# Four attention layers on one NeuronCore: the output projections and last stores of layers 2 and 3 moved into the branches, and eight additions of layer 1 handed to GpSimd

## The chip, the cores and the metric

The kernel runs on one core of a Trainium2 chip, in one launch. The metric is the device time in microseconds (us). Of the kernel before there are three runs: 3575.72, 3578.60 and 3578.97 us, median 3578.6. The profiled execution took 3578.05 us, and its profile spans 3576.3 us. All times below that are written as a position, such as 3514.46, are microseconds from the start of that span.

## The reference

An image x of shape (2, 512, 32, 32) goes through four layers. All data is float32. Only the ends of layers 1, 2 and 3 matter here:

```python
# layer 1: linear attention, residual
matrix_sum = v_sum[:, :, None] + jnp.einsum('bnm,bmc->bcn', Qt, matrix)
x = x + gamma[0] * (matrix_sum * tailor[:, None, :]).reshape(b, c, h, w)

# layers 2 and 3: group norm, q/k/v, attention of 8 heads of 64, projection, residual
xn = group_norm(x)                       # 8 groups in layer 2, 32 in layer 3
qkv = einsum('oc,bcn->bon', qkv_w, xn) + qkv_b
attn = softmax(q^T k * scale)            # per head, 1024 x 1024
out = einsum('bhnm,bhcm->bhcn', attn, v)
x = x + einsum('oc,bcn->bon', proj_w, out) + proj_b
```

## The kernel before

x stays on chip for the whole kernel: eight tiles `xs[b][t]` of 128 channels by 1024 positions, for two batches b and four channel blocks t. A "half" h below is 512 of the 1024 positions.

**Layer 0** (up to about 2107 us) is a deformable attention with a small network evaluated for each pair of positions, and then a two-matrix MLP (up to 2547 us). The change touches it only in names. One function of it, `share`, matters for the reading of the profile: it accumulates in one PSUM tile `acc` of 128 x 2 x 512 float32, writes half 0 with TensorE, has VectorE add it to x (line 202), and writes half 1.

**Layer 1** ends with 16 products, one for each batch, half and channel block (line 774), each 128 x 512 in PSUM. VectorE adds each to x (line 778). VectorE also takes the statistics for layer 2's group norm, two `bn_stats` for each tile of x (line 906) and one aggregation (907), for both batches, before layer 2's first product of q and k (848) can start.

**Layers 2 and 3** run through `attention`. `queries_keys_values` computes the group norm, q, k and v, and a flag that says whether the logits are small. Then the program branches at run time: `heads_bounded` does the softmax without a maximum, `heads_general` is the fallback. The data here take the bounded branch. In it, TensorE's order is written out by hand: 16 units (batch, pair of heads, half) of eight steps. In each step TensorE makes scores `s` (956), ScalarE takes the exponential (960), TensorE multiplies by v into `o` (985). VectorE and GpSimd add the exponentials up (965 to 974). At the end of a unit `divide` multiplies the sums by a matrix of ones into `d` (1002). ScalarE copies one half of `d` (1006), VectorE adds the other (1007), takes the reciprocal (1008) and scales the result q (1010). `divide` for a unit is called four steps into the next unit; for the last unit it is called after the last product by v, with nothing behind it in the branch.

After the branch, in code that both branches share, `project` runs 16 projections (batch, output block o, half): four matmuls of 128x128 by 128x512 into a one-bank PSUM tile `pb` (line 585; four such tiles rotate), and one VectorE instruction that adds bias and x (589). Each float32 matmul shows as two records in the profile. In layer 2 the statistics of layer 3's group norm (906, 907) stand in the same stretch of code, so they are placed between those additions. In layer 3, `epilogue` stores each tile of x once both halves are done (line 87, eight stores of 512 KB).

Outside the hand-written stretches a scheduler places instructions in each engine's queue, within one block of straight code; it does not move them across a branch. Waits between engines are semaphores. The program tracks a tile as a whole when it decides what has to wait for what.

Of the kernel before, what the change touches and what calls it, by code (L numbers as in the profile page):

```python
# [11 lines left out]
F32 = mybir.dt.float32  # L12
AF = mybir.ActivationFunctionType
ALU = mybir.AluOpType
# [4 lines left out]
P = 128  # L19
B, C, H, W = 2, 512, 32, 32  # L20
N = H * W
CT = C // P
# [25 lines left out]
class Net:  # L48
# [16 lines left out]
    def prologue(self, ctx: ExitStack):  # L65
# [13 lines left out]
                self.xs[b].append(xt)  # L79
        self.ident = const.tile([P, P], F32, tag="ident", name="ident")  # L80
        make_identity(nc, self.ident)

    def epilogue(self, out: bass.AP):
        y = out.rearrange("b (t p) h w -> b t p (h w)", p=P)
        for b in range(B):
            for t in range(CT):
                self.nc.sync.dma_start(y[b, t], self.xs[b][t])

# [7 lines left out]
    def layer0(self):  # L98
# [3 lines left out]
        with ExitStack() as ctx:  # L102
# [27 lines left out]
            with self.tc.manual_schedule(engines=engines):  # L130
                pairs = [{} for _ in range(BP)]
                for n, _ in enumerate(self.offsets(pairs[0], 0, ps)):
                    if n == 4:
                        self.fold_weights()
                front = [self.sampled(pairs[0], 0, ps)]
                after, sims, att = [], {}, None
                tables = {}
                quads = [(u, o, jj) for u in range(2 * BP) for o in range(8) for jj in range(2)]
                ready = self.first_hidden(*quads[0], pairs, tables)
                held, self.join = [], None  # L140
                for i, (u, o, jj) in enumerate(quads):
                    if o == 1 and jj == 1 and u % 2 == 0 and u // 2 + 1 < BP:
                        nxt = pairs[u // 2 + 1]
                        front += [self.offsets(nxt, u // 2 + 1, ps), self.sampled(nxt, u // 2 + 1, ps)]
                    h1 = ready
                    if i + 1 < len(quads):
                        if quads[i + 1][1:] == (7, 0) and u + 1 < 2 * BP:
                            self.advance(front, lambda: "logs" in pairs[(u + 1) // 2])
                        ready = self.first_hidden(*quads[i + 1], pairs, tables)
                    z = self.second_hidden(u, o, jj, h1, i + 1 == len(quads))  # L150
                    if jj == 1:
                        held.append((u, o, (first, z)))
                    else:
                        first = z
                        if len(held) == 2:
                            v, last, zs = held.pop(0)
                            self.last_product(v, last, zs, sims, ps_s)
                            if last == 7:
                                if v % 8 == 0:
                                    self.advance(after, lambda: False)  # L160
                                    att = [
                                        apool.tile([P, N], F32, tag=f"att{t}", name=f"att{v}_{t}") for t in range(CT)
                                    ]
                                self.advance(front, lambda: "v" in pairs[v // 2])
                                after.append(self.attend(v, pairs[v // 2], sims.pop(v), att, ps))
                                if v % 8 == 7:
                                    after.append(self.projection(ps, att, ow, v // 8))
                    self.step(after)
                    self.step(front)

                self.join(True)
                self.advance(after, lambda: False)
                self.last_product(*held[0], sims, ps_s)
                accs = [ps.tile([P, 2, HF], F32, tag="ps", name=f"ob{o}") for o in range(CT - 1)]
                share = self.share(accs, att, ow)
                next(share)
                self.last_product(*held[1], sims, ps_s)
                for n, _ in enumerate(self.attend(u, pairs[u // 2], sims.pop(u), att, None)):
                    if n in (0, 1):
                        next(share)  # L180
                for _ in share:
                    pass
                for h in range(2):
                    self.project_one(ps, att, ow, "out_b", B - 1, CT - 1, h)

    def share(self, accs, att, w):

# [63 lines left out]
    def projection(self, ps, att, ow, b):  # L251
        for o in range(CT):
            for h in range(2):
                self.project_one(ps, att, ow, "out_b", b, o, h)
                yield

    def offsets(self, m, bt, ps):
# [312 lines left out]
            nc.vector.tensor_copy(to[rows, HF:N], sim[rows, :])  # L570
        yield

    def project(self, ps, att, w, bias: str, b: int):

        for o in range(CT):
            for h in range(2):
                self.project_one(ps, att, w, bias, b, o, h)

    def project_one(self, ps, att, w, bias: str, b: int, o: int, h: int):
        nc = self.nc  # L580
        cut = slice(h * HF, (h + 1) * HF)
        acc = ps.tile([P, HF], F32, tag="ps", name=f"{bias}_{b}{o}{h}")
        for t in range(CT):
            wt = w[t] if isinstance(w, list) else w[:, t, :]
            nc.tensor.matmul(  # L585
                acc, lhsT=wt[:, o * P : (o + 1) * P], rhs=att[t][:, cut], start=(t == 0), stop=(t == CT - 1)
            )
        xt = self.xs[b][o][:, cut]
        nc.vector.scalar_tensor_tensor(xt, acc, self.col(bias, o), xt, ALU.add, ALU.add)
# [58 lines left out]
    def layer1(self, w, bias):  # L648
# [3 lines left out]
        with ExitStack() as ctx:  # L652
            pool = self.pool(ctx, "l1")
            small = self.pool(ctx, "l1s", 3)
            ps_t = self.pool(ctx, "l1_ps_t", 3, psum=True)
            ps_m = self.pool(ctx, "l1_ps_m", 1, psum=True)
            ps = self.pool(ctx, "l1_ps", 3, psum=True)
# [111 lines left out]
            for b in range(B):  # L769
                for h in range(2):  # L770
                    cut = slice(h * HF, (h + 1) * HF)
                    for t in range(CT):
                        w_ps = ps.tile([P, HF], F32, tag="ps", name=f"w{b}{h}{t}")
                        nc.tensor.matmul(
                            w_ps, lhsT=mats[b][:, t * P : (t + 1) * P], rhs=q_at[2 * b + h], start=True, stop=True
                        )
                        xt = self.xs[b][t][:, cut]
                        nc.vector.tensor_tensor(xt, w_ps, xt, ALU.add)

# [11 lines left out]
            proj.append(wt)  # L793
        return qkv, proj

    def attention(self, k: int, qkv, proj):
        nc = self.nc
        with ExitStack() as ctx:
            one = self.pool(ctx, f"a{k}")
            vb = one.tile([P, C], F32, tag="vb", name=f"vb{k}")  # L800
            nc.sync.dma_start(vb, self.io[f"l{k}_vb"].partition_broadcast(P))
            ones = one.tile([P, DH], F32, tag="ones", name=f"ones{k}")
            nc.vector.memset(ones, 1.0)
            data = []
            for b in range(B):
                qs = [one.tile([P, N], F32, tag=f"q{b}{t}", name=f"q{k}{b}{t}") for t in range(CT)]
                ks = [one.tile([P, N], F32, tag=f"k{b}{t}", name=f"k{k}{b}{t}") for t in range(CT)]
                v = one.tile([P, NB, C], F32, tag=f"v{b}", name=f"v{k}{b}")
                data.append((qs, ks, v))
            small_logits = self.queries_keys_values(k, qkv, vb, ones, data)  # L810

            with self.tc.If(small_logits > 0) as cmp:
                self.heads_bounded(k, ones, data)
            with cmp.Else():
                self.heads_general(k, data)
            with ExitStack() as ctx2:
                ps = self.pool(ctx2, f"a{k}_ps_p", 4, psum=True)
                for b in range(B):
                    self.project(ps, data[b][0], proj, f"pb{k}", b)

    def queries_keys_values(self, k, qkv, vb, ones, data):

# [107 lines left out]
            xn.append(xt)  # L930
        return xn

    def heads_bounded(self, k, ones, data):

# [4 lines left out]
        with ExitStack() as ctx:  # L941
# [72 lines left out]
            with self.tc.manual_schedule(engines={mybir.EngineType.PE}):  # L1014


                for i in range(len(steps) + 5):
                    if i < len(steps):
                        score(*steps[i])
                    for j in ([], [i - 3, i - 2])[i % NB == 3] if i % NB in (2, 3) else [i - 2]:  # L1020
                        if 0 <= j < len(steps):
                            value(*steps[j])
                    if i % NB == 4 and i > NB:
                        divide(steps[i - NB][0])

    def heads_general(self, k, data):
        with ExitStack() as ctx:
# [75 lines left out]
def conv_seq_kernel(ctx: ExitStack, tc: tile.TileContext, io: dict[str, bass.AP], out: bass.AP):  # L1103
# [3 lines left out]
    with tc.tile_pool(name="w_at", bufs=CT) as wpool:  # L1107
# [3 lines left out]
            l2 = net.attention_weights(wpool, 2)  # L1111
            net.layer1(*l1)
        net.attention(2, *l2)
        net.attention(3, *net.attention_weights(wpool, 3))
    net.epilogue(out)

# [107 lines left out]
```

## Time and profile before

| stretch, us | what runs | TensorE busy, us |
|---|---|---|
| 2546 to 2598 | layer 1 up to its last products | 50.6 of 52 |
| 2598 to 2624 | layer 1's additions, layer 2's group norm | 17.2 of 26 |
| 2624 to 2795 | layer 2: q, k, v | 168.9 of 171 |
| 2795 to 3037 | layer 2: heads | 236.1 of 242 |
| 3037 to 3099 | layer 2: projection, layer 3's group norm | 58.0 of 62 |
| 3099 to 3272 | layer 3: q, k, v | 170.5 of 173 |
| 3272 to 3514 | layer 3: heads | 235.4 of 242 |
| 3514 to 3576 | layer 3: projection, last store | 57.1 of 62 |

The table says how much of each stretch TensorE spent on matmuls; what is left over is time in which it waited. TensorE is the engine that is nearly always busy (3497.6 of 3576.3 us), so a change here acts on the time only through what it adds to, or takes from, TensorE's waits at the seams between these stretches, and through what follows the last matmul.

### The profile page before, as it was taken

Reading aid. Unit: us, or ns where it says so; the run is one execution under the profiler, and the core shown is the slowest. Engines: PE = TensorE matmul, PEld = TensorE weight load, DVE = VectorE, ACT = ScalarE, POOL = GpSimd, SP = SyncE. Lnnn points to the kernel's source line nnn. Section 1 sums busy time; section 2 is a strip of 40 time slices with the busy share of each in tenths; the row PEclk is TensorE's granted clock in tenths of the full one; section 3 lists DMA queues with packets and bytes.
Section 4 is the critical chain, followed back from the end, with each engine's and each line's share of the span. In section 5 each row is a group of like instructions: output and inputs, shape, how many; then the busy total and the mean of one; then the engine's idle time right before and its main releaser. Section 6 shows DMA issues by size and latency. Waiting matters only on the chain.

```text
span 3576.3 us, 58840 instructions
## 1 busy us (share of the span) xinstructions
PE 3497.6 (98%) x25184; PEld 1248.3 (35%) x25184; DVE 2023.0 (57%) x2075; ACT 1976.3 (55%) x2003; POOL 1869.8 (52%) x1392
## 2 busy tenths in 40 slices
PE   7999999999999999999999999999999999999998
PEld 2322332332323332332333334444644333443333
DVE  6877777767767668768766620000242467423674
ACT  5877787877776677777777720011010465102661
POOL 4878777787786687887788810000011344012441
PEclk9999999999999999999999999999999999999999
DMA  5777777787786687787888740000000000000001
GB/s 154 152 144 154 153 152 146 151 162 144 153 160 120 125 161 145 151 159 145 167 163 161 146 162 0 0 0 0 1 3 0 36 1 3 15 0 1 1 1 48
DMA packets 101799, 334.70 MB, mean 94 GB/s; under 512 B 12561, under 2 KB 14225, under 8 KB 100241
## 3 DMA queue, kind: packets, MB, share of 16 engines
q0 software_dynamic: 73296, 266.90, 39.4%
q1 hardware_dynamic: 27216, 61.82, 5.6%
q8 instruction: 202, 3.31, 0.4%
q10 hardware_dynamic: 1008, 2.06, 0.2%
q14 instruction: 77, 0.62, 0.1%
HBM read 59.40 MB, written 4.46 MB: 18 GB/s over the span
## 4 chain that ended last, share of the span: by engine, by line
PE 94%; DVE 5%; issue 1%; ACT 0%; POOL 0%; DMA 0%; DVEq 0%; ACTq 0%
PE hp L476 47%; PE m L619 6%; PE m L628 6%; PE s L956 6%; PE o L985 6%; PE qk0p L848 3%; PE pb L585 3%; PE qk1p L848 3%; PE sim L508 3%; PE vp L889 3%; DVE h L445 2%; DVE prod L278 1%; PE out_b L585 1%; PE d L1002 1%; DVE conv L291 1%; PE ob L193 1%
## 5 line engine op out<-in xcount | busy, mean ns | idle before, releaser
L476 PE MATMUL hp<-h,w 128*32 128x512 f32 x16384 | 1825.1, 593 | 7.4 <-DVE h L445 5.9
L445 DVE CUSTOM_DVE_ANT_1 h<-tx,bank 128x1024 f32<-128x1024 f32 x1024 | 1180.9, 1215 | 344.8 <-PE hp L476 321.7
L481 ACT ACTIVATE h<-hp,magb 128x1024 f32<-128x1024 f32 x1024 | 1123.7, 1112 | 437.1 <-PE hp L476 436.1
L476 PEld LDWEIGHTS hp<-h,w 128*32 128x32 f32 x16384 | 529.6, 110 | 1233.2 <-issue 1151.6
L468 POOL DMA_DIRECT2D h<-h x509 | 452.7, 1026 | 406.7 <-ACT h L487 348.5
L494 POOL TENSOR_TENSOR h<-h,h 128x1024 f32<-128x1024 f32 x255 | 614.6, 2410 | 21.3
L492 POOL TENSOR_SCALAR h<-h,flip 128x1024 f32<-128x1024 f32 x256 | 448.9, 1754 | 0.9 <-ACT h L481 0.9
L960 ACT ACTIVATE e<-s 128x1024 f32<-128x1024 f32 x256 | 258.7, 1024 | 152.7 <-PE s L956 152.6
L483 ACT ACTIVATE h<-h,flip 128x1024 f32<-128x1024 f32 x256 | 291.3, 1138 | 0.0
L956 PE MATMUL s<-q,k 64*64 64x512 f32 x2048 | 259.9, 590 | 5.1 <-ACT e L960 3.4
L985 PE MATMUL o<-e,v 64*64 64x512 f32 x2048 | 260.8, 592 | 0.0
L659 POOL MEMSET l1ones<- 128x128 f32 x1 | 0.2, 205 | 476.0 <-PE m L628 476.0
L623 ACT ACTIVATE mh<-m,cols 128x512 f32<-128x512 f32 x64 | 44.0, 687 | 336.5 <-PE m L619 336.5
L619 PE MATMUL m<-mx,w 128*128 128x512 f32 x512 | 220.5, 592 | 0.9 <-issue 0.9
L628 PE MATMUL m<-mh,w 128*128 128x512 f32 x512 | 220.4, 592 | 0.0
L967 POOL TENSOR_TENSOR some<-some,e 128x1024 f32<-128x1024 f32 x64 | 151.3, 2364 | 82.5 <-ACT e L960 80.0
L636 DVE SCALAR_TENSOR_TENSOR x<-m,cols,x 128x512 f32<-128x512 f32 x16 | 12.0, 750 | 318.0 <-PE m L628 318.0
L485 POOL TENSOR_SCALAR h<-h,flip 128x1024 f32<-128x1024 f32 x128 | 154.5, 1207 | 64.0 <-ACT h L481 62.8
L965 POOL TENSOR_TENSOR some<-e,e 128x1024 f32<-128x1024 f32 x32 | 75.9, 2371 | 212.6 <-ACT q L994 139.2
L862 POOL TENSOR_TENSOR sq<-q 128x1024 f32<-128x1024 f32 x16 | 30.3, 1894 | 280.3 <-DVE q L856 280.3
L860 ACT ACTIVATE k<-qk1p,cols 128x512 f32<-128x512 f32 x32 | 22.0, 687 | 245.0 <-PE qk1p L848 245.0
L487 ACT ACTIVATE h<-h,flip 128x1024 f32<-128x1024 f32 x128 | 145.6, 1138 | 0.0
(206 smaller groups left out, 2708.0 us busy)
## 6 DMA issues: line engine op xcount, KB each, us to landing
h<-h POOLq DMA_DIRECT2D x509, 512.0 KB, 6.5
lb<-logs SPq DMA_DIRECT2D x63, 512.0 KB, 5.2
w<-in_mlp_w SPq DMA_DIRECT2D x8, 1024.0 KB, 11.7
qkv<-in_l_qkv SPq DMA_DIRECT2D x8, 768.0 KB, 5.7
x<-in_x SPq DMA_DIRECT2D x8, 512.0 KB, 9.6
out<-x SPq DMA_DIRECT2D x8, 512.0 KB, 2.6
proj<-in_l_proj SPq DMA_DIRECT2D x8, 256.0 KB, 5.9
l1w<-in_l_w SPq DMA_DIRECT2D x1, 1280.0 KB, 8.2
```

The lines of the kernel that those rows point to most:

```text
L445: self.nc.vector._custom_dve(TENSOR_ADD_SAT, out=h[:, k, :, :], in0=x[:, jj, 2 * r + k, :].unsqueeze(1).to_broadcast([P, H, W]), in1=y[:, ...
L468: nc.gpsimd.dma_start(to, what, accum_op=ALU.add)
L476: nc.tensor.matmul(hp[rows, cut], lhsT=self.l0w2[:, 32 * q : 32 * q + 32], rhs=h1[k][:, cut], start=True, stop=True)
L481: nc.scalar.activation(y, hp, AF.Relu, bias=self.magb[:, q : q + 1])
L483: nc.scalar.activation(ys[0], ys[0], AF.Copy, scale=self.flip[:, 0:1])
L492: nc.gpsimd.tensor_scalar(y, y, self.flip[:, 2:3], 1.0, ALU.mult, ALU.mult)
L494: (nc.vector if final else nc.gpsimd).tensor_tensor(y, y, ys[2], ALU.add)
L619: nc.tensor.matmul(acc, lhsT=w1[t][:, o * P : (o + 1) * P], rhs=xn[t], start=(t == 0), stop=(t == CT - 1))
L628: nc.tensor.matmul(acc, lhsT=w2[t // 4][:, t % 4, o * P : (o + 1) * P], rhs=hs[t], start=(t == 0), stop=(t == nh - 1),)
L956: nc.tensor.matmul(s[halves[c], par, :], lhsT=ks[p][rows, at : at + DH], rhs=qs[p][rows, cut], start=True, stop=True)
L960: nc.scalar.activation(e, s, AF.Exp)
L985: nc.tensor.matmul(o[halves[par], r, :], lhsT=v[rows, n, at : at + DH], rhs=e[rows, par, :], start=(n == 0), stop=(n == NB - 1),)
```

## The change

It does four things:

1. Layer 1: for batch 1, ScalarE copies each product out of PSUM into one of four buffers `ws`, and GpSimd adds it to x. Batch 0 stays on VectorE. This relieves VectorE, which both adds and takes statistics there.
2. Layers 2 and 3: the projection moves from behind the branch into both branches, so that it can follow the heads without a jump in between.
3. In the bounded branch the first projection block (batch 0, output block 0, both halves) runs ahead of the last `divide`, whose sums are then given time to become ready; batch 0 does not need that last unit.
4. Each projection block takes one PSUM tile of two halves, from the two buffers that the scores use, instead of two one-bank tiles from a set of four. The last stores are issued half by half (16 of 256 KB) in the branch.

```diff
     def project_one(self, acc, att, w, bias, b, o, h):     # acc is now passed in
-        acc = ps.tile([P, HF], F32, tag="ps", name=f"{bias}_{b}{o}{h}")
...
+    def project_block(self, acc, att, w, bias: str, b: int, o: int, out):
+        for h in range(2):
+            cut = slice(h * HF, (h + 1) * HF)
+            self.project_one(acc[:, h, :], att, w, bias, b, o, h)
+            if out is not None:
+                self.nc.sync.dma_start(out[b, o][:, cut], self.xs[b][o][:, cut])
...
 # layer1
+            last = self.pool(ctx, "l1w", 4)
...
-                        nc.vector.tensor_tensor(xt, w_ps, xt, ALU.add)
+                        if b == 0:
+                            nc.vector.tensor_tensor(xt, w_ps, xt, ALU.add)
+                        else:
+                            ws = last.tile([P, HF], F32, tag="ws", name=f"ws{h}{t}")
+                            nc.scalar.copy(ws, w_ps)
+                            nc.gpsimd.tensor_tensor(xt, xt, ws, ALU.add)
...
 # attention
             with self.tc.If(small_logits > 0) as cmp:
-                self.heads_bounded(k, ones, data)
+                self.heads_bounded(k, ones, data, proj, out)
             with cmp.Else():
                 self.heads_general(k, data)
-            with ExitStack() as ctx2:
-                ps = self.pool(ctx2, f"a{k}_ps_p", 4, psum=True)
-                for b in range(B):
-                    self.project(ps, data[b][0], proj, f"pb{k}", b)
+                with ExitStack() as ctx2:
+                    ps = self.pool(ctx2, f"a{k}_ps_p", 2, psum=True)
+                    for b in range(B):
+                        for o in range(CT):
+                            acc = ps.tile([P, 2, HF], F32, tag="ps", name=f"pbg{k}{b}{o}")
+                            self.project_block(acc, data[b][0], proj, f"pb{k}", b, o, out)
...
 # heads_bounded, behind the loop over steps
-                    if i % NB == 4 and i > NB:
+                    if i % NB == 4 and NB < i < len(steps):
                         divide(steps[i - NB][0])
+                for b in range(B):
+                    for o in range(CT):
+                        acc = ps_s.tile([P, 2, HF], F32, tag="s", name=f"pb{k}{b}{o}")
+                        self.project_block(acc, data[b][0], proj, f"pb{k}", b, o, out)
+                        if b == o == 0:
+                            divide(units[-1])
```

More of the change, by code (lines that the diff above doesn't have):

```diff
@@ L81, in prologue @@
         make_identity(nc, self.ident)
-    def epilogue(self, out: bass.AP):
-        y = out.rearrange("b (t p) h w -> b t p (h w)", p=P)
-        for b in range(B):
-            for t in range(CT):
-                self.nc.sync.dma_start(y[b, t], self.xs[b][t])
     def bn(self, pool, which: str):
@@ L183, in layer0 @@
                 for h in range(2):
-                    self.project_one(ps, att, ow, "out_b", B - 1, CT - 1, h)
+                    acc = ps.tile([P, HF], F32, tag="ps", name=f"out_b_end{h}")
+                    self.project_one(acc, att, ow, "out_b", B - 1, CT - 1, h)
     def share(self, accs, att, w):
@@ L253, in projection @@
             for h in range(2):
-                self.project_one(ps, att, ow, "out_b", b, o, h)
+                acc = ps.tile([P, HF], F32, tag="ps", name=f"out_b{b}{o}{h}")
+                self.project_one(acc, att, ow, "out_b", b, o, h)
                 yield
@@ L571, in attend, with project_one @@
         yield
[L573 to L579, printed above, removed]
+    def project_block(self, acc, att, w, bias: str, b: int, o: int, out):
[4 more added lines that the diff above has]
+                self.nc.sync.dma_start(out[b, o][:, cut], self.xs[b][o][:, cut])
+    def project_one(self, acc, att, w, bias: str, b: int, o: int, h: int):
         nc = self.nc
         cut = slice(h * HF, (h + 1) * HF)
-        acc = ps.tile([P, HF], F32, tag="ps", name=f"{bias}_{b}{o}{h}")
         for t in range(CT):
@@ L794, in attention_weights, with attention @@
         return qkv, proj
-    def attention(self, k: int, qkv, proj):
+    def attention(self, k: int, qkv, proj, out=None):
         nc = self.nc
@@ L812, in attention @@
             with self.tc.If(small_logits > 0) as cmp:
-                self.heads_bounded(k, ones, data)
+                self.heads_bounded(k, ones, data, proj, out)
             with cmp.Else():
                 self.heads_general(k, data)
-            with ExitStack() as ctx2:
-                ps = self.pool(ctx2, f"a{k}_ps_p", 4, psum=True)
-                for b in range(B):
-                    self.project(ps, data[b][0], proj, f"pb{k}", b)
+                with ExitStack() as ctx2:
[4 more added lines that the diff above has]
+                            self.project_block(acc, data[b][0], proj, f"pb{k}", b, o, out)
     def queries_keys_values(self, k, qkv, vb, ones, data):
@@ L931, in group_norm, with heads_bounded @@
         return xn
-    def heads_bounded(self, k, ones, data):
+    def heads_bounded(self, k, ones, data, proj, out):
         nc = self.nc
@@ L1113, in conv_seq_kernel @@
         net.attention(2, *l2)
-        net.attention(3, *net.attention_weights(wpool, 3))
-    net.epilogue(out)
+        net.attention(3, *net.attention_weights(wpool, 3), out.rearrange("b (t p) h w -> b t p (h w)", p=P))
 def _per_partition(v):
```

## The prediction

> **What bounds the kernel now.** I read the chain of waits on the page first, then the timeline at the four seams the edit touches, then the granted clock there. The chain:
>
> ```profile
> PE 94%; DVE 5%; issue 1%; ACT 0%; POOL 0%; DMA 0%; DVEq 0%; ACTq 0%
> ```
>
> TensorE (PE) carries 94% of it, and the number of matmuls does not change. So I price only the time in which TensorE stands still. End of layer 3's heads, by the timeline:
>
> ```profile
> 3505.21 2.75 PE L985 MATMUL o<-e,v 64*64 64x512 f32 x24
> ...
> 3510.44 1.09 PE L1002 MATMUL d<-sum,ones 64*64 64x512 f32 x8 [2.47 <-DVE sum L974]
> 3511.59 0.59 ACT L1006 COPY r<-d 128x512 f32<-128x512 f32 x1 [2.98 <-PE d L1002]
> 3512.21 0.69 DVE L1007 TENSOR_TENSOR r<-d,r 128x512 f32<-128x512 f32 x1 [1.23 <-ACT r L1006]
> 3512.94 3.35 DVE L1008 RECIPROCAL r<-r 128x512 f32<-128x512 f32 x1
> 3514.46 6.05 PE L585 MATMUL pb<-q,proj 128*128 128x512 f32 x9 [2.94 <-issue]
> ```
>
> Two holes: 2.47 us for the last sum, then 2.94 that nothing in the program explains ("issue"), across the jump to the shared code. And nine records take 6.05 us where the steady pace is 0.43 each (one projection, eight records, is 3.43: its additions at L589 come every 3.43). The clock, by stretches (columns: the stretch, its length, busy time and count of TensorE, weight loads, VectorE, ScalarE and GpSimd, then the granted clock, the DMA share and GB/s):
>
> ```profile
> 3514.00:3516.00 2.00, 1.54 (x2) 0.84 (x3) 2.00 (x1) 0.00 (x0) 0.00 (x0) 0.50 0.04 12
> 3516.00:3518.00 2.00, 2.00 (x3) 0.67 (x2) 0.98 (x2) 0.00 (x0) 0.00 (x0) 0.50 0.01 4
> 3518.00:3520.00 2.00, 2.00 (x6) 0.98 (x5) 0.00 (x0) 0.00 (x0) 0.00 (x0) 0.90 0.01 4
> ```
>
> After the holes the clock is 0.50 for some 4 us; 3514.46 to the first addition at 3520.12 is 5.66 us for 3.43 of work. Layer 2's seam shows the same: sum wait 2.47, issue 1.73, slow start.
>
> From layer 2 to layer 3, statistics of x lie between the additions and cost nothing:
>
> ```profile
> 3090.53 0.75 DVE L589 SCALAR_TENSOR_TENSOR x<-pb,cols,x 128x512 f32<-128x512 f32 x1 [1.71 <-PE pb L585]
> 3091.31 0.69 DVE L906 BATCH_NORM_STATS2 stats<-x 128x6 f32<-128x512 f32 x1
> ...
> 3099.41 5.49 PE L848 MATMUL qk0p<-xn,qkv 128*128 128x512 f32 x6 [1.93 <-ACT xn L929]
> ```
>
> The projection's matmuls end at 3093.93, so that seam is 5.5 us. Last, layer 0's `share` accumulates two halves in one tile, as the edit's blocks will:
>
> ```profile
> 2090.68 1.13 PE L193 MATMUL ob<-att,ow 128*128 128x512 f32 x2 [0.66 <-ACT att L569]
> 2091.84 0.75 DVE L202 SCALAR_TENSOR_TENSOR x<-ob,cols,x 128x512 f32<-128x512 f32 x1 [1.06 <-PE ob L193]
> 2092.65 1.98 PE L193 MATMUL ob<-att,ow 128*128 128x512 f32 x4 [0.84 <-DVE x L202]
> ```
>
> TensorE stops 0.84 us before half 1, until VectorE has read half 0, though the halves are different columns.
>
> [...] here 2.36 us (L967) against 1.23 (L974) for 128x1024.
>
> **The change, part by part.** H is the end of the heads' last product (3030.99 in layer 2, 3507.96 in layer 3), P the end of the projection's matmuls.
>
> *Heads to P.* Removed from TensorE's path, layer 3: 2.47 + 2.94 + 2.2 of slow clock (5.66 - 3.43) = 7.6 us. Layer 2: 2.47, a d that takes 1.80 for 1.09 (0.7), 1.73, and 3036.99 to 3043.01 for 3.43 (2.6) = 7.5.
> Added: in the built program's order every half 1 waits on VectorE and, from the third block on, no half 0 does. That is consistent only with half 1 waiting for the addition of half 0 of its own block, as in `share`. Eight blocks at 0.84 = 6.7 us a layer. In the second block it is longer. From H: half 0 to 3.43, stall to 4.27, half 1 to 7.70, d to 8.57, half 0 of block 1 to 12.00. VectorE's queue holds L1007 and L1008 ahead of that block's first addition: 8.57 + 0.6 (ACT) + 0.7 + 3.4 = 13.3, addition to 14.06, half 1 from 14.12. Stall 2.12. So block 1 ends at 17.55, and six blocks of 6.87 + 0.84 bring P to H + 63.8. Before it was 3571.60 - 3507.96 = 63.6 in layer 3 and 62.9 in layer 2. Net **+0.2 and +0.9**: the holes are traded for stalls. The sum, ready 2.43 after H, is hidden by half 0; the last scaling of q (14.8) is first needed in the fifth block, at H + 33. What queues behind half 1's wait on TensorE is the rest of the projection, so each stall goes straight into P. The 16 stores issue from an idle queue beside it.
>
> *Layer 2 to layer 3.* The statistics now lie behind the branch, all after the last addition. VectorE: jump 2.8 to 3.9 us from its last dispatch (ACT took 2.75 from L1006 to its next instruction, TensorE 4.0 from d to pb); I take first statistics at P + 3.3. Eight `bn_stats` and four aggregations: at layer 1's end four and two took 2.51 (2613.05 to 2615.56), so 5.0, to P + 8.3. Then the group norm's chain, by the rows of the seams before: 0.8 over the mean product to its copy (L909, L911), 0.75 for three steps of the variance (2623.74 to 2624.48), 0.6 over the variance product to L919 (2618.62 to 2619.24), 0.9 over the root to the first xn (3096.38 to 3097.30), 2.1 over ScalarE's bias to the product (3097.30 to 3099.41): P + 13.4 against 5.5. TensorE waits through it, where before all but the chain's last part lay beside the projection. And TensorE's order puts one matmul of batch 0 there, then the mean product of batch 1, which needs batch 1's statistics; VectorE does these after four xn (2.98) and seven more `bn_stats` (4.7). That gives P + 19.5 for the second matmul. With 0.4 for the variance product and the clock still at half rate for about three matmuls (1.72 each), the first eight matmuls end near P + 27.6. Before: 3099.41 + 10.09 = P + 15.6, slow clock included. **+12.0.** Bounds: +9 if the jump is hidden[...].
>
> *Layer 1 to layer 2.* VectorE loses 8 additions of about 0.66 (L778). GpSimd's 128x512 addition isn't in the trace. From below, half of 2.36 is 1.18; from above, VectorE's addition is 1.23 for 128x1024 and 0.69 for 128x512, half and 12%, so 1.4. I take 1.2. The first product of batch 1 ends at 2606.2 (2598.43 and nine times 0.86), the copy (0.6, as L994) lies on a ScalarE idle there, the first addition starts near 2607.05, and eight end at 2616.7. What queues behind them is VectorE: the statistics of batch 1 wait for GpSimd, and behind those waits stand the steps of batch 0's norm (mean copy, variance), on which the first q product depends. TensorE's order also puts both variance products ahead of that product now; before, batch 1's lay behind it. From 2616.7: last statistics to 2617.4, variance product and scale of batch 0 to 2619.3, first xn at 2619.6 against 2620.89. **-1.0** with margin rounded off; at 1.4 the additions end 1.6 later, +0.5.
>
> *End.* The last store is half as large. 512 KB land in 2.6 us, so I take 2.3: -0.3. VectorE's jump,[...] ends 2.0 to 3.1 us after the last addition, against that. **0**, bounds -0.3 and +0.6.
>
> Sum: 0.2 + 0.9 + 12.0 - 1.0 + 0 = +12.1: **3590.7 us**, 0.34% slower.
>
> **The rivals.** (a) As intended: no half waits, no exposed statistics: -7.5 - 7.5 - 1.0 = -16, 3562.6. For it: the holes are real. Against: `share` shows the wait, and statistics cannot cross a branch. Chance 5%. (b) Statistics exposed, but no half-tile stall: -1.0 + 12.0 + (0.9 - 6.7 - 1.3) + (0.2 - 6.7 - 1.3) = -3.9, 3574.7, no measurable change. Against it again `share`. 7%. (c) Stalls as priced, but the seam costs half ([...] batch 1's statistics short of blocking): +6, 3584.6. 10%. (d) The same as my forecast, with [...] a cold clock for longer: +17, 3595.6. 8%. My forecast: 70%.
>
> **How the numbers follow.** The forecast's own bounds are 3586 to 3594. Leaving out (a) and (b) leaves 12%; the range is 3582 to 3596 with (c) and (d). The line for "slower" is 3585.8: forecast and (d) are above, (c) mostly within 0.2%. Slower 0.80, same 0.14, faster 0.06.
>
> **What would show it.** Right: L589's line of waits shows pb waiting 0.8 us on VectorE once a block, 2.1 in the second; no "issue" ahead of pb and its clock at 1.0; `bn_stats` of layer 3 in one run behind the last addition, and about 13 us without projections or q products; a second hole of 4 to 5 us after the first q matmul. Wrong: halves of a block back to back, or statistics among the additions.

## The result, and the profile after

The changed kernel takes 3596.95 us (median of 6 runs, 3595.27 to 3598.37); the kernel before, in runs beside it, 3576.85 us. The ratio is 1.0055, with a 95% interval of 1.0042 to 1.0068: half a per cent slower. The two profiles span 3595.5 and 3576.3 us, 19.2 apart. The forecast was 3590.7 us with a range of 3582 to 3596, so the direction was right and the cost was put too low.

The chain of waits of the kernel after says that the bound is the same engine. TensorE's share is a point smaller than before, and "issue" (time in which an engine waits for nothing that the profile shows) has fallen from 1% to 0%:

```profile
PE 93%; DVE 5%; POOL 1%; ACT 0%; issue 0%; DMA 0%; DVEq 0%; ACTq 0%
```

The heads' end in layer 2, TensorE alone, in the timeline of the kernel after (start, duration, engine, line, operation, count, and in brackets the idle time ahead of it with what ended it):

```profile
3027.58 2.75 PE L994 MATMUL o<-e,v 64*64 64x512 f32 x24
3030.27 3.70 PE L583 MATMUL pb<-q,proj 128*128 128x512 f32 x8
3034.81 3.70 PE L583 MATMUL pb<-q,proj 128*128 128x512 f32 x8 [0.85 <-DVE x L587]
3038.44 1.09 PE L1011 MATMUL d<-sum,ones 64*64 64x512 f32 x8
3039.46 3.70 PE L583 MATMUL pb<-q,proj 128*128 128x512 f32 x8
3044.92 7.13 PE L583 MATMUL pb<-q,proj 128*128 128x512 f32 x16 [1.76 <-DVE x L587]
3052.90 7.13 PE L583 MATMUL pb<-q,proj 128*128 128x512 f32 x16 [0.84 <-DVE x L587]
```

The intended gain is there: the projection follows `o` without a hole, the product of ones `d` takes 1.09 us and waits for nothing, and the granted clock is 1.00 from 3028 to 3044. The price stands in the brackets. Eight records, one half of a block, run; TensorE stops until VectorE has read that half; then half 1 of this block and half 0 of the next run as one row of 16. In the second block VectorE is busy with the reciprocal when half 0 is done, so the stop is 1.76 us, as VectorE's timeline of the kernel after shows:

```profile
3040.94 3.35 DVE L1017 RECIPROCAL r<-r 128x512 f32<-128x512 f32 x1
3044.21 0.65 DVE L587 SCALAR_TENSOR_TENSOR x<-pb,cols,x 128x512 f32<-128x512 f32 x1
```

Over the kernel, the list of TensorE's waits puts this line first (us in total, times, longest):

```profile
PE pb L583 <- DVE x L587: 15.3, 16, 1.8
```

Sixteen waits: eight blocks in each of two layers, 14 of 0.84 or 0.85 and two of 1.76.

"Jump" stands below for an engine's passage from the end of the branch to the code that both branches share. At the seam from layer 2 to layer 3 the timeline of the kernel after shows, on VectorE, the jump (2.83 us) and then the statistics in one run,

```profile
3096.53 0.75 DVE L587 SCALAR_TENSOR_TENSOR x<-pb,cols,x 128x512 f32<-128x512 f32 x1 [3.79 <-PE pb L583]
3100.11 1.29 DVE L915 BATCH_NORM_STATS2 stats<-x 128x6 f32<-128x512 f32 x2 [2.83 <-issue]
```

and on TensorE the wait that they cause, and the second one:

```profile
3092.79 3.70 PE L583 MATMUL pb<-q,proj 128*128 128x512 f32 x8 [0.85 <-DVE x L587]
3106.07 0.56 PE L918 MATMUL gm<-mv,avg 128*128 128x4 f32 x2 [9.58 <-DVE mv L916]
3107.47 0.59 PE L926 MATMUL gv<-dv,avg 128*128 128x4 f32 x2 [0.85 <-DVE dv L924]
3111.12 2.08 PE L857 MATMUL qk0p<-xn,qkv 128*128 128x512 f32 x2 [3.06 <-ACT xn L938]
3117.11 0.59 PE L918 MATMUL gm<-mv,avg 128*128 128x4 f32 x2 [3.91 <-DVE mv L916]
3119.69 6.60 PE L857 MATMUL qk0p<-xn,qkv 128*128 128x512 f32 x12
```

TensorE waits 9.58 us for the first mean product `gm`, whose input is the end of the statistics, and 3.91 us for that of batch 1. In the kernel before, the same stretch on TensorE was

```profile
3028.24 2.75 PE L985 MATMUL o<-e,v 64*64 64x512 f32 x24
3036.99 56.93 PE L585 MATMUL pb<-q,proj 128*128 128x512 f32 x128 [1.73 <-issue]
3099.41 10.09 PE L848 MATMUL qk0p<-xn,qkv 128*128 128x512 f32 x16 [1.93 <-ACT xn L929]
```

So the 19.2 us divide as follows. H is the end of the heads' last product and P the end of the projection, as in the prediction; "q" is the end of the first eight calls (matmuls of the program, two records each) of layer 3's q product, where the next row begins: 3109.33 before, 3126.12 after.

| stretch | before, us | after, us | difference | predicted |
|---|---|---|---|---|
| start of the span to H of layer 2 | 3030.99 | 3030.33 | -0.7 | -1.0 |
| H to P, layer 2 | 62.94 | 66.16 | +3.2 | +0.9 |
| P to q | 15.40 | 29.63 | +14.2 | +12.0 |
| q to H of layer 3 | 398.63 | 398.63 | 0.0 | 0 |
| H to P, layer 3 | 63.64 | 66.16 | +2.5 | +0.2 |
| P of layer 3 to the end | 4.70 | 4.59 | -0.1 | 0 |
| sum | | | +19.1 | +12.1 |

### The profile page after: what moved, and what is told of

It is laid out like the page before. It is cut to its first block, busy times and chain, and to the rows that moved or that the text cites. A ratio compares the mean times of both kernels' runs of the same rounds, so it can differ in the third digit from the quotient of the medians.

```text
span 3595.5 us, 58867 instructions
## 1 busy us (share of the span) xinstructions
PE 3498.6 (97%) x25184; PEld 1245.4 (35%) x25184; DVE 2015.9 (56%) x2067; ACT 1980.1 (55%) x2011; POOL 1875.9 (52%) x1400
## 4 chain that ended last, share of the span: by engine, by line
PE 93%; DVE 5%; POOL 1%; ACT 0%; issue 0%; DMA 0%; DVEq 0%; ACTq 0%
PE hp L472 47%; PE o L994 6%; PE m L617 6%; PE m L626 6%; PE s L965 6%; PE qk0p L857 3%; PE qk1p L857 3%; PE pb L583 3%; PE sim L504 3%; PE vp L898 3%; DVE h L441 2%; DVE prod L274 1%; PE out_b L583 1%; PE d L1011 1%; DVE conv L287 1%; PE ob L188 1%
```

## The experiments

Theory: the time goes to two places, the stop in each block, because one tile holds both halves, and the statistics, because they can no longer lie between the additions. The rivals: the stop is something else than the tile; the seam is the jump alone; the removed holes had cost nothing. The median of the kernel before, run beside each group of experiments, lay between 3576.3 and 3579.2 us. Ratios are against those runs. A difference from the kernel after, which was timed with the first result only, is therefore good to about 3 us; the finer readings are those of the traces.

**1. The tile alone (e1_tile).** The kernel before, with only its PSUM tile changed to that of the edit.

```diff
+            acc = ps.tile([P, 2, HF], F32, tag="ps", name=f"{bias}_{b}{o}")
             for h in range(2):
-                self.project_one(ps, att, w, bias, b, o, h)
+                self.project_one(ps, att, w, bias, b, o, h, acc[:, h, :])
...
-                ps = self.pool(ctx2, f"a{k}_ps_p", 4, psum=True)
+                ps = self.pool(ctx2, f"a{k}_ps_p", 2, psum=True)
```

> The kernel before, with one edit: the projections behind the branch take one tile of two halves from two buffers, instead of one-bank tiles from four. Theory (the half-tile wait): each of 16 blocks stands 0.84 us for VectorE and loses another 0.27 us [...], 1.11 together, 17.8 in sum: 3576.9 + 17.8 = 3594.7 us, with no other seam moved. Rival (what slows the projection in the changed kernel is that it lies in the branch: [...] its clock): the tile alone costs nothing, 3576.9, within 3.

Measured: 3578.5 us, ratio 1.0004 (0.9995 to 1.0012). The theory missed. In the timeline of TensorE in layer 3 of this kernel,

```profile
3512.84 53.74 PE L587 MATMUL pb<-q,proj 128*128 128x512 f32 x120 [2.37 <-issue]
3567.43 3.70 PE L587 MATMUL pb<-q,proj 128*128 128x512 f32 x8 [0.84 <-DVE x L591]
```

120 records run without a stop, and only the last half waits, 0.84 us. This stretch of code is ordered by the scheduler. What it does can be read from VectorE's additions: in layer 2 of this kernel the second, third and fourth start at 3046.68, 3048.40 and 3053.55, 1.72 and 5.15 us apart, where those of the kernel before lie 3.43 apart from 3045.89 on. That is the spacing that four records of another block between the two halves of one tile give. In the branch, TensorE's order is the order in which the code is written. So the tile alone does not make the stops. What remains is an order that writes the two halves of a tile one behind the other, and the branch as a rival; experiment 2 tells these apart.

**2. The tile and the order, without the branch (e5_hand).** Experiment 1 with TensorE's order in the projection fixed to the written one.

```diff
-                for b in range(B):
-                    self.project(ps, data[b][0], proj, f"pb{k}", b)
+                with self.tc.manual_schedule(engines={mybir.EngineType.PE}):
+                    for b in range(B):
+                        self.project(ps, data[b][0], proj, f"pb{k}", b)
```

> The kernel before, with the two-half tiles of the first experiment, and TensorE's order of the projection fixed by hand as in the changed kernel. Theory: the tile costs time only where the order is fixed, since the scheduler otherwise puts another block's matmuls between the two halves; with the order fixed, 16 blocks at 1.11 us = 17.8, 3577.9 + 17.8 = 3595.7 us, with a wait of 0.84 us on VectorE at each half 1. Rival (the stall needs the branch, not the order): 3578, as with the tile alone.

Measured: 3588.85 us, ratio 1.0029 (1.0018 to 1.0041). The stops are there without the branch, at their price, in the timeline of TensorE in layer 2 of this kernel:

```profile
3059.66 7.13 PE L587 MATMUL pb<-q,proj 128*128 128x512 f32 x16 [0.85 <-DVE x L591]
3067.64 7.13 PE L587 MATMUL pb<-q,proj 128*128 128x512 f32 x16 [0.85 <-DVE x L591]
3074.61 0.28 PE L912 MATMUL gm<-mv,avg 128*128 128x4 f32 x2
3075.62 7.13 PE L587 MATMUL pb<-q,proj 128*128 128x512 f32 x16 [0.73 <-DVE x L591]
3082.59 0.28 PE L920 MATMUL gv<-dv,avg 128*128 128x4 f32 x2
```

From H to P layer 2 takes 73.17 us (+10.2 over before) and layer 3 72.13 (+8.5). The time went up by less than their sum because the seam into layer 3 shrank from 15.40 to 8.43 us: with TensorE's order written out, the mean and variance products of batch 0 (`gm`, `gv`) fell between projection blocks, so q's input was ready at the end of the projection. 10.2 + 8.5 - 7.0 = +11.7; the spans differ by 10.8, since the heads of layer 2 end 0.9 us earlier here than in the kernel before, with the same code up to there. The expectation (3595.7) had not seen that coupling. It says that the seam of the kernel before had about 7 us to give.

**3. The same tile, another order (e2_pairs).** The kernel after, with two blocks projected in turns, so that no half stands directly behind the other half of its tile.

```diff
-                    for o in range(CT):
-                        acc = ps_s.tile([P, 2, HF], F32, tag="s", name=f"pb{k}{b}{o}")
-                        self.project_block(acc, data[b][0], proj, f"pb{k}", b, o, out)
-                        if b == o == 0:
-                            divide(units[-1])
+                    for o in (0, 2):
+                        accs = [ps_s.tile([P, 2, HF], F32, tag="s", name=f"pb{k}{b}{o + i}") for i in range(2)]
+                        for h in range(2):
+                            for i in range(2):
+                                self.project_half(accs[i], data[b][0], proj, f"pb{k}", b, o + i, h, out)
+                                if b == o == h == i == 0:
+                                    divide(units[-1])
```

> The changed kernel, with one edit: two blocks are projected in turns (half 0 of block A, half 0 of block B, half 1 of A, half 1 of B), so that each half 1 starts one projection after its tile's half 0. Theory: heads to last projection falls from 66.2 us to 16 x 3.43 + 0.87 + 0.3 = 56.1 in each layer, 20 us in all: 3577 us; the seam from layer 2 to layer 3 stays as long as in the changed kernel, 29.6 us from the last projection to the end of the first eight q products. Rival (branch code is slow as such): 3597, unchanged.

Measured: 3577.5 us, ratio 1.0000 (0.9991 to 1.0009), 19.5 below the kernel after. In the timeline of TensorE of this kernel all projections behind `d` are one row with no bracket:

```profile
3030.42 3.70 PE L589 MATMUL pb<-q,proj 128*128 128x512 f32 x8
3034.05 1.09 PE L1017 MATMUL d<-sum,ones 64*64 64x512 f32 x8
3035.07 51.77 PE L589 MATMUL pb<-q,proj 128*128 128x512 f32 x120
```

H to P of layer 2 falls from 66.16 to 56.35 us, by 9.8; the seam behind it hardly moves (29.95). With tile, pool and branch as they were, the order takes the stops away; the last `divide` moves too, by one half block, and `d` waits for nothing in either place. This run also shows what the edit was after. Without the stops, H to P is 6.6 and 7.3 us shorter than in the kernel before, so the removed holes did cost time. The seam is 14.6 us longer, and that cancels it.

**4. The statistics in the branch (e3_stats).** The kernel after, with the statistics of layer 3 taken in layer 2's branches, behind each block.

```diff
                         self.project_block(acc, data[b][0], proj, f"pb{k}", b, o, out)
+                        self.next_stats(b, o)       # two bn_stats, one bn_aggr into tiles kept for layer 3
```

> The changed kernel, with one edit: the statistics of layer 3's group norm are taken in layer 2's branches, behind each block. Theory (exposed statistics): the first q product comes about 9 us after the last projection instead of 14.6 (last statistic 1.7, jump 2.8, norm chain 4.5), the second hole of 3.9 us is gone, and the first eight q products end near 19 us instead of 29.6: 3597 - 10.5 = 3586.5 us. Rival (the jump and the cold clock are the loss, the statistics would be hidden by them): 3595 or more.

Measured: 3587.25 us, ratio 1.0025 (1.0014 to 1.0037), 9.7 below the kernel after. The seam falls from 29.63 to 19.82 us. What remains of the jump is in VectorE's timeline of this kernel:

```profile
3097.22 0.21 DVE L584 BATCH_NORM_AGGREGATE mvn<-nstats 128x2 f32<-128x12 f32 x1
3100.91 0.16 DVE L930 COPY gms<-gm 128x4 f32<-128x4 f32 x1 [3.48 <-issue]
```

VectorE stands 3.48 us at the jump while the mean product (from 3096.04) has long been done, and TensorE waits 5.33 us for the variance's input. So of the seam's 14.2 us, 9.8 are statistics out of place. Against the 15.40 before, 4.4 remain; the jump of 3.48 us, which now has nothing beside it, lies in them, and the rest is not separated here. Experiment 8 puts the jump back beside matmuls.

**5. The first block's place (e4_order).** The kernel after, with the last divide ahead of the first block, as in the kernel before.

```diff
-                    if i % NB == 4 and NB < i < len(steps):
+                    if i % NB == 4 and i > NB:
...
-                        if b == o == 0:
-                            divide(units[-1])
```

> The changed kernel, with one edit: the last product of ones stands ahead of the first projection block again, inside the branch. Theory: the wait of 2.5 us for the last sum is back in each layer, and the long stall behind the reciprocal moves from the second block to the first without getting shorter: +2.5 a layer, 3602 us; no issue hole of 2 to 3 us and no slow clock behind it. Rival (the place of that product doesn't matter, since the reciprocal holds up a projection either way): 3597.

Measured: 3603.3 us, ratio 1.0072 (1.0055 to 1.0089), 6.3 above the kernel after: 3.1 a layer (H to P of layer 2 is 69.23 for 66.16). The time is near the expected 3602; two parts of its reasoning did not hold. The long stop behind the reciprocal is gone and not moved: every stop is now 0.84 us. And in TensorE's timeline of this kernel the clock did drop, behind a hole of 2.47 us alone:

```profile
3031.98 1.66 PE L1011 MATMUL d<-sum,ones 64*64 64x512 f32 x8 [2.47 <-DVE sum L983]
3033.57 4.78 PE L583 MATMUL pb<-q,proj 128*128 128x512 f32 x8
```

`d` took 1.66 us for 1.09 and the first half block 4.78 for 3.70; the granted clock was 0.59 from 3032 to 3034 and 0.55 to 3036. So the placement is a gain, as the edit meant, and part of its worth is the clock: 2.47 for the hole and 0.57 + 1.08 for the slow records make 4.12; less 0.92, since the second block now stops for 0.84 and not 1.76, that is 3.2 for the 3.07 measured.

**6. Layer 1's part alone (e8_layer1)**, in the kernel before.

```diff
+                            nc.scalar.copy(ws, w_ps)
+                            nc.gpsimd.tensor_tensor(xt, xt, ws, ALU.add)     # batch 1 only
```

> The kernel before with layer 1's part of the change alone. Theory: the first xn of layer 2 comes 0.6 us earlier, as in the changed kernel, and the whole is shorter by as much, which is too little for the times to show: 3575.7 us of span. Rival (it is worth more or less without the rest of the change): the end of layer 2's heads moves by another amount than 0.66 us.

One run: 3577.5 us, span 3575.7 against 3576.3. That is no more than the scatter of runs. The trace tells more: from the start of layer 1's last products to layer 2's first xn it is 21.82 us here and in the kernel after, and 22.46 in the kernel before (22.46 and 22.47 in experiments 1 and 2, which lack this part). So the part is worth 0.64 us up to there. How much of it reaches the end of the heads is not shown: with the same code, that end lies at 3030.99 in the kernel before and at 3029.79 and 3030.09 in experiments 1 and 2. Eight additions on GpSimd show as one row in the timeline of this kernel, 1.23 us each:

```profile
2607.53 9.84 POOL L785 TENSOR_TENSOR x<-x,ws 128x512 f32<-128x512 f32 x8 [42.03 <-ACT ws L784]
```

**7. Both cures (e6_both).** Experiments 3 and 4 in one kernel.

> The changed kernel with both edits, blocks in turns and statistics in layer 2's branches. Theory: the two gains add up, 3597 - 20 - 10 = 3567 us: heads to last projection 56.3 us in each layer, and from there 20 us to the end of the first eight q products, 4.5 more than before. Rival (one hides behind the other, or VectorE, which now has statistics between the additions, holds up the halves again): 3572 or more.

Measured: 3567.6 us, ratio 0.9966 (0.9955 to 0.9978). The two add up: 3596.95 - 19.5 - 9.7 = 3567.8, and H to P (56.35) is that of experiment 3. This is the edit with its two costs taken away, as far as the branch allows; the seam is still 19.6 us, in TensorE's timeline of this kernel,

```profile
3094.93 0.59 PE L942 MATMUL gv<-dv,avg 128*128 128x4 f32 x2 [6.26 <-DVE dv L940]
```

because VectorE's jump (3.8 us in this kernel) stands between the last statistics and the norm.

**8. Half of layer 2's projection behind the branch (e7_split).** Experiment 3, and in layer 2 the branches project batch 0 only. Batch 1 follows behind them in tiles of one half each, among layer 3's statistics, so that VectorE's jump lies beside matmuls.

```diff
-                    for b in range(B):                                       # in both branches
+                    for b in range(B if out is not None else 1):
...
+            if out is None:                                                  # behind them, layer 2 only
+                with ExitStack() as ctx2:
+                    ps = self.pool(ctx2, f"a{k}_ps_l", 4, psum=True)
+                    for o in range(CT):
+                        for h in range(2):
+                            acc = ps.tile([P, HF], F32, tag="ps", name=f"pbl{k}{o}{h}")
+                            self.project_one(acc, data[B - 1][0], proj, f"pb{k}", B - 1, o, h)
```

> The changed kernel with blocks in turns, and in layer 2 only batch 0 projected in the branches; batch 1 is projected behind them, with one-bank tiles, among the statistics of layer 3. Theory: the jump and batch 0's statistics lie beside batch 1's projection, so that the seam is as short as before (15.4 us from the last projection to the end of the first eight q products) and the heads end 7 us earlier in both layers: 3577.9 - 0.7 - 7 - 7.3 = 3563 us. Rival (TensorE's own jump now stands between the two parts of the projection and costs 2 to 3 us and some slow clock): 3567.

Measured: 3564.7 us, ratio 0.9959 (0.9946 to 0.9973). VectorE's jump is there, 2.09 us, with matmuls beside it. TensorE's own jump, which the rival had priced at 2 to 3 us, does not show: TensorE stands 0.84 us behind the branch, and for VectorE's last addition:

```profile
3058.50 27.73 PE L589 MATMUL pbl<-q,proj 128*128 128x512 f32 x64 [0.84 <-DVE x L593]
```

The seam is 14.6 us, near the 15.40 of the kernel before; against experiment 7 it is 5.0 shorter.

**9. The norm's first half earlier (e9_early).** Experiment 8, with what experiment 2 showed by accident done on purpose: the mean and variance products of batch 0 stand between projection blocks of batch 1.

```diff
...
+                    norm = self.norm_scale(3, 0, self.avg3, self.sp, psg)
+                    with self.tc.manual_schedule(engines={mybir.EngineType.PE}):
                         for o in range(CT):
                             for h in range(2):
                                 acc = ps.tile([P, HF], F32, tag="ps", name=f"pbl{k}{o}{h}")
                                 self.project_one(acc, data[B - 1][0], proj, f"pb{k}", B - 1, o, h)
+                            if o in (1, 2):
+                                self.early = next(norm)
...
```

> The kernel is e7_split with the group means and variances of layer 3's first batch computed in layer 2's tail: their two small matmuls stand, in an order of TensorE written by hand, behind the second and third pair of projection blocks of the second batch, so that the first product of layer 3 finds its input ready. My reading of e5 is that the seam between layers 2 and 3 is set by where these two products stand; there they stood among the projection's blocks and the seam, from the end of the projection to the end of the first eight calls of q, was 8.4 us. Theory: the seam falls from 14.6 us in e7_split to about 8.4, and the time from 3564.7 to about 3558.5 us. Rival: VectorE's jump and the eight statistics of the first batch come so late in the tail that the mean product waits for them and TensorE with it, the blocks behind it too; the hole moves ahead of the end of the projection and the time stays at 3564 us or more.

Measured: 3557.2 us (3557.12 to 3558.24), ratio 0.9946 (0.9933 to 0.9960). In TensorE's timeline of this kernel the two products and the blocks behind them wait for nothing, and the first q product waits 0.89 us:

```profile
3073.52 0.28 PE L935 MATMUL gm<-mv,avg3e 128*128 128x4 f32 x2
3073.66 7.11 PE L589 MATMUL pbl<-q,proj 128*128 128x512 f32 x16
3080.61 0.28 PE L944 MATMUL gv<-dv,avg3e 128*128 128x4 f32 x2
3080.75 7.11 PE L589 MATMUL pbl<-q,proj 128*128 128x512 f32 x16
3088.76 1.95 PE L875 MATMUL qk0p<-xn,qkv 128*128 128x512 f32 x4 [0.89 <-ACT xn L962]
```

The projection ends at 3087.86 and the first eight calls of q at 3096.30: 8.4 us, as expected. This version is 0.54% faster than the kernel before and about 1.1% faster than the kernel after.

It also bears on the stops. Batch 1's projection has TensorE's written order here, half 1 behind half 0 of each block, as in experiment 2, but with four tiles of one half each. No half of it stops; its first row shows only the wait behind the branch:

```profile
3059.68 14.00 PE L589 MATMUL pbl<-q,proj 128*128 128x512 f32 x32 [0.84 <-DVE x L593]
```

The tile alone (experiment 1) leaves one stop a layer, this order alone none; both together (experiment 2, and the kernel after) stop in every block.

## Why the prediction was right in direction and too small

**The stop in each block: the right mechanism, one term too small.** The waits stand where they were placed (one a block, 1.76 us for 2.12 in the second), and the seam, the additions of layer 1 and the end all moved as described. The step that failed is the size of one term, "eight blocks at 0.84". 0.84 is the idle time that the profile records, not what TensorE loses. In the kernel after, half 0 of the first block starts at 3030.27 and half 1 at 3034.81, 4.54 us apart where the pace is 3.43: the stop costs **1.11**. The missing 0.27 is hidden in the row's duration: eight records show as 3.70 us, while in experiment 3's row 120 of them take 51.77, or 0.43 each and 0.27 once. Behind a record that others follow, the next starts 0.43 us later; ahead of a stop, these 0.27 us come on top and count as busy. What they consist of, the trace does not show. The term was readable before: the prediction's lines of `share` start at 2090.68 and 2092.65, so two records and one stop take 1.97 us; less two times 0.43, that is 1.11.

Seven stops of this kind at 0.27 are 1.9 of the 2.3 us that each layer came out above the forecast. Another 0.27 is the recorded end of the last row, which the sum to P left out while the 63.6 and 62.9 before contain it. Of the rest, the rows round `d` took 0.35 longer (3.63 and 1.02 us for 3.43 and 0.87), and the second block's stop, 2.03 us from start to start for 2.12, took a little back. The same 0.27 is in the reading of the slow clock: at full pace a half needs 3.74 us and not 3.43 from its first record to its addition (3030.27 to 3034.01 in the kernel after), so the slow starts cost about 1.9 and 2.3 us, not 2.2 and 2.6. The forecast does not rest on that; rival (a) does.

**The seam: the right chain, each link a little short.** By the trace of the kernel after, first statistics at P + 3.6 (3.3), statistics 5.7 (5.0), from there to the first q product 5.3 (5.1), to the second call 6.4 (6.1), to the end of eight calls 8.6 (8.1), against a seam before of 15.4 (15.6): 0.3 + 0.7 + 0.2 + 0.3 + 0.5 + 0.2 = 2.2 us. The largest link is the statistics, where one tile took 1.4 us in this run of eight and 1.25 in the stretch of layer 1 from which the price came; why is not shown. The clock was 0.50 from 3102 to 3122 by the windows, under the last links; how much of their excess is its doing is not separated.

**The rest.** Layer 1's part came to -0.7 in the table for -1.0. Up to the first xn it is 0.65 us, where the sum had 1.3: the additions ended where they were placed (2616.85 for 2616.7), and the statistics behind them at 2618.4 for 2617.4. GpSimd's addition is 1.23 us for the 1.2 taken. At the end, 256 KB land in 2.0 us for the 2.3 taken (median of 16), and the total there is -0.1 for 0; what took the difference back is not shown. The exchange of holes for stops came out as a loss of 2.5 to 3.2 us a layer and not as a near tie.

**The rivals.** That the edit works as intended (3562.6) and that no half stops (3574.7) are refuted by the rows above; experiment 3, which takes the stops away, is where the second would have been, at 3577.5. Half the seam's cost (3584.6, with +6 at the seam) is refuted by the +14.2 of the table. The fourth rival, with a longer jump at both ends and a slow clock for longer (3595.6), came nearest in time, by luck; why either would be longer was not shown. Of the 7.0 us that the forecast missed, 4.6 lie between H and P, where this case had added nothing; its share is at most 0.3 of jump and 0.5 in the last link. VectorE's first statistics start 3.6 us behind the start of its last addition, inside the 2.8 to 3.9 that the forecast allowed, and the end of layer 3 cost nothing.

**One reason was incomplete.** The prediction put the stop down to the two halves of a block lying in one tile. Experiment 1 has the same tiles and hardly a stop: it also takes an order that leaves nothing to do between the two halves, which the built program had and a scheduled stretch did not.

## What to carry to other kernels

When an order is written by hand, put the halves of one PSUM tile apart, with another tile's work between them (experiment 3, 9.8 us less from H to P), or give each half a tile of its own (experiment 9, where no half stopped). Price a stop by the distance between the starts of the rows ahead of and behind it, less the steady pace, because the recorded idle time of TensorE left out 0.27 of 1.11 us here. Before moving work into a branch, list what its neighbours were hiding: here VectorE's statistics and its jump lay beside the projection, and outside they cost as much as the closed holes had (14.6 against 13.9 us in experiment 3). At this seam, the first product of the next stage was set by the small products ahead of it, and their place in TensorE's queue, between blocks of the stage before, was worth 6 us (14.6 to 8.4).

## What the runs showed of the hardware beside that

In layer 2 of experiment 5 a hole of 2.47 us on TensorE was enough to lower the granted clock: no second hole follows it, and the clock was 0.59 and 0.55 for the 4 us behind it, where the 16 records took 1.65 us longer. The product behind such a hole was not always slow: in layer 2 of experiment 2, behind 2.48 us, it took 1.09 us, as it does at a clock of 1.00 in the kernel after. What decides this is not shown.

What a jump costs differs by engine and by what stands ahead of it. VectorE stands 2.1 to 3.8 us at the end of layer 2's branch: 2.09 in experiment 8, 2.21 in 9, 2.83 in the kernel after, 3.2 in experiment 3, 3.4 in 5, 3.48 in 4, 3.8 in 7. TensorE shows a hole of 1.73 to 2.94 us where it had just waited for the last sum (the kernel before and experiments 1, 2 and 6). Where a projection runs ahead of the jump it shows next to none: the mean product behind it starts 0.37 us after the projection in experiment 4, and without a hole in experiment 7. The cause of the differences is not shown.
